# Proj's products split by seven a second time, and half of the exchange issued from GpSimd's queue

## The chip, the cores and the metric

The kernel runs on one core of a Trainium2 chip. The metric is device time in microseconds for one execution. TensorE is called PE (its weight loads PEld), VectorE DVE, ScalarE ACT, GpSimd POOL and SyncE SP.

## What is computed

A cross-attention block, all in fp32, for four batches of 512 queries and 512 context rows, width 512, 16 heads of 32, MLP width 2048:

```python
x = layer_norm(hidden_states, ln1_w, ln1_b)
q = x @ q_w + q_b;  k = ctx @ k_w + k_b;  v = ctx @ v_w + v_b
attn = softmax(q k^T / sqrt(32), masked)
hidden = (attn v) @ cproj_w + cproj_b + hidden_states
y = layer_norm(hidden, ln2_w, ln2_b)
y = gelu(y @ fc_w + fc_b)
return hidden + y @ proj_w + proj_b
```

## The kernel before

**An order written out.** The string ORDER holds some thousands of tokens, and a loop at the end issues them one after another. A token such as `P:0:5` names a step (here project, batch 0, product 5); a step that yields is taken up again where it stopped when its token comes again. Each engine works its instructions strictly in this order, and so do the DMA queues: `load` (L278) puts a DMA on SP's queue, `nc.gpsimd.dma_start` one on POOL's. The tiles of a Ring (`accs`, four PSUM banks; `stage`, two SBUF buffers; `rows_of`, six) are taken and given back in this order as well. `add` (L281) and `sub` (L284) are helpers, so sums of many places share these lines.

**Attention** runs over 16 groups w (batch and four heads) and four query tiles. Token `u` (L419) makes scores into four PSUM banks `sc`, `x` subtracts the minimum on DVE (L427) and exponentiates on ACT (L430), `r` transposes 32x32 blocks on DVE into `swap` (L438, L445). `e` is the exchange: for each half of a group 16 DMAs, each of a 32-partition block of 136 KB, put the transposed blocks into the partitions where `a` (attend, L470) needs them:

```python
for d in range(NI):
    for i in (0, 2, 1, 3):
        j = (i + d) % NI
        load(pT[ts(j, HD), i], tb[ts(i, HD), j])
    yield
```

Between these stand the products of k, q and v (L384, L396, L406) for later groups, c (cproj, L352), the layer norms (`s`, `r1`, `r2`, `n`, `t`) and fc.

**fc** (L528) is a Strassen-Winograd product: for each batch b and each of eight pairs c of blocks of 128 hidden columns (`f:b:c`) seven products in place of eight. `fs` makes the four sums of its weights on POOL (for the last batch `sw`, on DVE), `j` (fc_join) joins the seven results into a stage buffer, `g` applies gelu on ACT (L575). The result of the first three batches goes to DRAM (`gd`, L578, on POOL's queue) and comes back for proj; that of the last batch (`z`, `zj`, `zg`) stays in SBUF.

**proj** (`P:b:n`, L637) is 512 rows by 2048 by 512 for each batch, again in seven products n of 256x1024 by 1024x256: 16 matmul calls of 256 columns each. `ps` makes the weight sums once, `gs` the sums of the activations on DVE (the rows of L281 and L284 that name `swap` and `mix`), `J` (project_join) adds the results into the residual, which `hd` loads and to which `pb` adds the bias on POOL, and stores the output. Products 1, 2 and 6 use the ring of accumulators, the rest the four score banks, which are free by then.

An fp32 matmul call shows as two instructions in the profile.

Of the kernel before, what the change touches and what calls it, by code (L numbers as in the profile page):

```python
# [12 lines left out]
F32 = mybir.dt.float32  # L13
# [27 lines left out]

LN1W, LN1B, QB, KB, LN2W, LN2B, FCB = 0, 4, 8, 12, 16, 20, 24
# [24 lines left out]
u:2:0 k:4 e:1:0 e:1:0 e:1:0 r:1:3 s1:1 r1:1 n1:1 a:0:1 r:1:2 x:2:0 n1:1 n1:1 r:1:3 x:2:0 x:2:0 x:2:0 n1:1 r:1:3 k:5
u:2:1 x:2:1 wk:6 wq:4 wq:5 x:2:1 r:2:0 k:4 x:2:1 e:1:1 e:1:1 e:1:1 wk:7 e:1:1 v:4 x:2:1 r:2:0 t1:1:0
u:2:2 r:2:1 x:2:2 t1:1:1 t1:1:1 r:2:1 t1:1:0 x:2:2 r:2:1 r:2:1 x:2:2 x:2:2 v:5 t1:1:2 t1:1:2 a:1:0
u:2:3 a:1:0 x:2:3 v:5 t1:1:3 t1:1:3 x:2:3 q:5 a:1:1 r:2:2 x:2:3 x:2:3 r:2:2 r:2:3 a:1:1  # L70
u:3:0 k:6 k:6 x:3:0 r:2:3 r:2:3 x:3:0 r:2:3 x:3:0 x:3:0 q:5 e:2:0 wv:7 e:2:0 e:2:0 e:2:0 q:4
u:3:1 x:3:1 x:3:1 r:3:0 r:3:1 x:3:1 x:3:1 v:4 r:3:1 r:3:1 r:3:0 r:3:1 k:7
u:3:2 a:2:0 x:3:2 q:4 e:2:1 e:2:1 e:2:1 wq:7 e:2:1 a:2:0 e:3:0 e:3:0 e:3:0 x:3:2 x:3:2 wv:6 wq:6 e:3:0 x:3:2 v:7
u:3:3 q:7 r:3:2 r:3:2 x:3:3 x:3:3 a:2:1 x:3:3 x:3:3 r:3:3 r:3:3 v:7
u:4:0 m:1 x:4:0 x:4:0 x:4:0 x:4:0
u:4:1 r:3:3 a:2:1 r:3:3 k:7 x:4:1 e:3:1 e:3:1 x:4:1 r:4:0 x:4:1 x:4:1 r:4:1 r:4:1 r:4:0 e:3:1 e:3:1 r:4:1 q:6 a:3:0
  a:3:0
u:4:2 x:4:2 x:4:2 r:4:1 x:4:2 x:4:2 c:0:1 v:6
u:4:3 c:0:1 v:6 x:4:3 e:4:0 e:4:0 lh:0 e:4:0 e:4:0 lx:2 le:2 lh:0 le:2 le:2 wk:8 wv:8 le:2 r:4:2 c:0:0 x:4:3 x:4:3
  x:4:3  # L80
u:5:0 a:3:1 c:0:0 r:4:3 r:4:2 x:5:0 x:5:0 q:6 x:5:0 x:5:0 a:3:1 c:0:2 fs:0:0 cb:0 c:0:0 r:4:3 s2:0
u:5:1 r:4:3 c:0:2 v:4 v:5 cb:0 x:5:1 r:4:3 q:7 r:5:0 x:5:1 x:5:1 x:5:1 c:0:3 c:0:3 a:4:0
u:5:2 v:8 k:8 s2:0 s2:0 s2:0 r:5:1 r:5:0 a:4:0 c:0:1 fs:0:0 c:0:2 c:0:3 r2:0 x:5:2 x:5:2 n2:0 n2:0 n2:0 n2:0 t2:0:0
  t2:0:0 x:5:2 v:8 r:5:1 t2:0:1 x:5:2 t2:0:1
u:5:3 t2:0:3 t2:0:2 r:5:1 wk:9 e:4:1 x:5:3 t2:0:3 k:9 x:5:3 k:9 t2:0:2 r:5:1 s1:2 e:4:1 e:4:1 e:4:1 r:5:2 x:5:3 wv:9
  a:4:1 lh:1 x:5:3 r:5:2
u:6:0 r:5:3 a:4:1 x:6:0 k:8 y:0 y:0 lx:2 s1:2 lx:2 s1:2 lx:2 s1:2 y:0 e:5:0 wv:10 wq:8 e:5:0 e:5:0 e:5:0 wk:10 f:0:1
  v:9 f:0:0 v:9 j:0:0 r1:2 x:6:0 r:5:3 x:6:0 r:5:3 n1:2 n1:2 f:0:0 f:0:1 f:0:0 j:0:0 n1:2 n1:2 x:6:0 r:5:3 y:0 e:5:1
  e:5:1 lh:1 e:5:1 lf:0:4 wq:9
u:6:1 j:0:0 j:0:0 t1:2:2 x:6:1 j:0:1 t1:2:2 r:6:0 x:6:1 f:0:0 x:6:1 x:6:1 j:0:0 t1:2:0 t1:2:0 g:0:0 g:0:0 a:5:0  # L90
u:6:2 t1:2:1 r:6:0 a:5:0 j:0:1 r:6:1 k:10 x:6:2 t1:2:1 r:6:1 x:6:2 x:6:2 x:6:2 r:6:1 t1:2:3 f:0:1 t1:2:3
u:6:3 r:6:1 e:5:1 j:0:1 x:6:3 x:6:3 r:6:2 x:6:3 j:0:1 x:6:3 r:6:3 r:6:3 k:10 q:9 a:5:1 a:5:1 r:6:2
u:7:0 x:7:0 x:7:0 fs:0:3 g:0:0 fs:0:2 q:9 r:6:3 fs:0:2 f:0:2 fs:0:3 fs:0:1 fs:0:2 fs:0:2 f:0:2 f:0:1 j:0:2 x:7:0 x:7:0
  j:0:1 g:0:1 g:0:1 g:0:1 cb:1 fs:0:3 fs:0:3 r:6:3 j:0:2 lx:3 e:6:0 e:6:0 e:6:0 lf:0:4 e:6:0 f:0:3 f:0:2
u:7:1 f:0:2 j:0:2 j:0:2 j:0:2 g:0:2 g:0:2 g:0:2 v:6 x:7:1 x:7:1 r:7:0 j:0:3 r:7:0 q:8 f:0:3 x:7:1 x:7:1 j:0:3 a:6:0
u:7:2 v:7 r:7:1 a:6:0 x:7:2 v:10 x:7:2 x:7:2 q:8 r:7:1 r:7:1 v:10 x:7:2 r:7:1 e:6:1 lh:1 m:1 cb:1 fs:0:4 v:9 cb:1 v:8
  fs:0:4 fs:0:4 fs:0:4 e:6:1 e:6:1 e:6:1 r:7:2 wq:11 wv:11 e:7:0 wq:10
u:7:3 f:0:4 j:0:4 x:7:3 x:7:3 f:0:4 j:0:4 x:7:3 r:7:2 x:7:3 f:0:3 a:6:1
u:8:0 m:2 v:11 x:8:0 r:7:3 x:8:0 v:11 x:8:0 j:0:3 r:7:3 r:7:3 f:0:4 j:0:3 a:6:1 j:0:4 x:8:0 f:0:3
u:8:1 r:7:3 wk:11 lf:0:6 lf:1:0 e:7:0 e:7:0 e:7:0 lf:0:5 wv:13 lf:0:5 e:7:1 f:0:4 lh:1 e:7:1 q:10 wq:12 e:7:1 lf:0:7  # L100
  e:7:1 r:8:0 x:8:1 x:8:1 j:0:4 x:8:1 j:0:4 a:7:0 j:0:3 x:8:1
u:8:2 r:8:1 g:0:3 a:7:0 r:8:1 g:0:3 r:8:0 r:8:1 x:8:2 x:8:2 g:0:4 g:0:4 x:8:2 c:1:0 r:8:1 lf:0:7 lf:1:0 e:8:0 e:8:0
# [97 lines left out]
def xattn_block(ctx: ExitStack, tc: tile.TileContext, x, encT, mask, q_w, k_w, v_w, c_w, w_fc, p_w, vecs, rows, out):  # L200
# [577 lines left out]
```

## Time and profile before

| | |
|---|---|
| median of 3 runs | 791.18 us (789.69 to 792.59) |
| profiled execution | 789.92 us |
| its span | 788.1 us, granted clock 1.00 |
| busy in the span: PE, DVE, ACT, POOL | 778.2, 565.9, 361.0, 188.6 us |
| DMA | 158.16 MB, mean 201 GB/s |
| scores run | 22.9 to 502 us |
| first product of proj | 541 us |
| last matmul ends, last join | 785, 785.4 us |

Busy time of PE includes time in which matmuls wait in the pipeline, so 99% does not say that it is full. The chain of waits is the sequence of work that ended last, followed back from the last instruction. A group's row gives line, engine, operation, tiles out<-in, shapes and count, then busy us and mean ns of one, then idle us before it with what ended the idle time. A DMA on POOL's or SP's queue shows there with the time of its issue, and in the list of issues with the time until it landed.

### The profile page before, as it was taken

How to read it: one execution, taken by the hardware profiler on the slowest of the kernel's cores; microseconds unless marked ns; L12 is line 12 of the kernel's file. 1: busy time of each engine (PE TensorE's matmuls, PEld its weight loads, DVE VectorE, ACT ScalarE, POOL GpSimd, SP SyncE). 2: the span in 40 equal slices, each digit the busy share in tenths (PEclk: the TensorE clock that was granted, in tenths of full speed). 3: DMA queues.
4: the chain of work that ended last, by engine and by line, in shares of the span. 5: the costliest groups of instructions: out<-in, count | busy, mean ns of one | idle time of the engine just before them, and what ended most of it. 6: DMA issues, size and time to landing. Idle time of an engine off the chain costs nothing.

```text
span 788.1 us, 12510 instructions
## 1 busy us (share of the span) xinstructions
PE 778.2 (99%) x4370; PEld 538.2 (68%) x4370; DVE 565.9 (72%) x1145; ACT 361.0 (46%) x764; POOL 188.6 (24%) x230
## 2 busy tenths in 40 slices
PE   9998999999999999999999999999999999999998
PEld 6543653557566556665546677766888888888887
DVE  3788879899988799997889898844963248532631
ACT  2565755556865765859587777920000010112000
POOL 0141000220271133303232724400142600110411
PEclk9999999999999999999999999999999999999999
DMA  8988878898989989887977998899804602300003
GB/s 296 298 212 212 235 186 203 238 289 206 255 230 250 260 231 265 252 248 191 264 215 204 278 290 235 220 269 412 317 1 161 226 27 66 115 28 1 27 7 107
DMA packets 64031, 158.16 MB, mean 201 GB/s; under 512 B 12848, under 2 KB 17072, under 8 KB 62304
## 3 DMA queue, kind: packets, MB, share of 16 engines
q1 hardware_dynamic: 58992, 140.36, 63.2%
q0 software_dynamic: 4832, 16.98, 5.8%
q8 instruction: 35, 0.57, 0.3%
q14 instruction: 28, 0.23, 0.1%
q10 hardware_dynamic: 144, 0.02, 0.0%
HBM read 65.03 MB, written 20.97 MB: 109 GB/s over the span
## 4 chain that ended last, share of the span: by engine, by line
PE 91%; DMA 2%; DVE 2%; ACT 2%; SPq 2%; issue 0%; POOL 0%; DVEq 0%; POOLq 0%
PE acc L528 20%; PE sc L637 14%; PE acc L637 11%; PE sc L419 8%; PE acc L384 7%; PE acc L470 7%; PE acc L406 7%; PE acc L396 6%; PE acc L352 6%; PE sc L528 4%; PE acc L320 2%; DMA swap<-swap 2%; SPq L278 2%; DVE ptt L427 1%; ACT ptt L430 1%; DMA ext<-fc_w_dram 1%
## 5 line engine op out<-in xcount | busy, mean ns | idle before, releaser
L430 ACT ACTIVATE ptt<-ptt,mn 128x512 f32<-128x512 f32 x256 | 182.7, 715 | 105.9 <-DVE mn L427 105.2
L427 DVE CUSTOM_DVE_ANT_0 ptt<-sc,mix 128x512 f32<-128x512 f32 x256 | 165.4, 678 | 27.8 <-PE sc L419 23.6
L438 DVE STREAM_TRANSPOSE swap<-ptt 128x1024 f32<-128x1024 f32 x64 | 78.9, 1234 | 9.0 <-DMA pbt<-fc_w_dram 3.9
L419 PE MATMUL sc<-pbt 32*128 32x512 f32 x512 | 80.0, 640 | 1.6 <-ACT pbt L398 0.8
L445 DVE STREAM_TRANSPOSE swap<-ptt 128x1024 f32<-128x1024 f32 x64 | 77.9, 1222 | 1.2 <-ACT ptt L430 1.2
L470 PE MATMUL acc<-swap,mix 128*32 128x256 f32 x1024 | 61.9, 382 | 3.1 <-DMA swap<-swap 3.1
L406 PEld LDWEIGHTS acc<-ptt,ext 128*128 128x128 f32 x512 | 58.9, 192 | 7.0 <-issue 4.2
L528 PE MATMUL acc<-yT,pbt 128*128 128x256 f32 x240 | 62.5, 389 | 0.3 <-DVE st L281 0.2
L406 PE MATMUL acc<-ptt,ext 128*128 128x128 f32 x512 | 60.8, 277 | 0.0
L528 PEld LDWEIGHTS acc<-yT,pbt 128*128 128x128 f32 x240 | 43.4, 190 | 23.1 <-issue 9.8
L384 PE MATMUL acc<-ext,ptt 128*128 128x512 f32 x128 | 58.7, 604 | 0.0
L352 PE MATMUL acc<-mix 128*128 128x512 f32 x128 | 58.5, 599 | 0.1
L396 PE MATMUL acc<-ext,ptt 128*128 128x512 f32 x128 | 58.2, 599 | 0.0
L528 PE MATMUL acc<-ys,wsum 128*128 128x256 f32 x224 | 57.6, 379 | 0.3 <-DVE ys L284 0.3
L637 PE MATMUL acc<-pbt,swap 128*128 128x256 f32 x256 | 57.0, 379 | 0.0
L470 PEld LDWEIGHTS acc<-swap,mix 128*32 128x32 f32 x1024 | 30.2, 109 | 38.6 <-issue 9.9
L637 PEld LDWEIGHTS acc<-pbt,swap 128*128 128x128 f32 x256 | 48.6, 190 | 7.0 <-DVE mix L281 0.2
L281 POOL TENSOR_TENSOR xn<-xn,row 128x512 f32<-128x512 f32 x16 | 20.4, 1274 | 135.4 <-DMA xn<-x_dram 135.3
L281 DVE TENSOR_TENSOR st<-acc,st 128x512 f32<-128x512 f32 (+1 forms) x72 | 42.2, 593 | 12.9 <-PE acc L528 11.5
L654 ACT COPY mix<-acc 128x512 f32<-128x512 f32 x4 | 2.3, 586 | 100.0 <-PE acc L637 42.8
L430 ACT ACTIVATION_READ_ACCUMULATOR ptt<-ptt,mn 128x1 f32 x256 | 48.0, 188 | 0.0
L528 PEld LDWEIGHTS acc<-ys,wsum 128*128 128x128 f32 x224 | 42.5, 190 | 6.4 <-issue 0.7
(107 smaller groups left out, 1205.4 us busy)
## 6 DMA issues: line engine op xcount, KB each, us to landing
swap<-swap SPq DMA_DIRECT2D x512, 136.0 KB, 3.3
gd<-st POOLq DMA_DIRECT2D x24, 512.0 KB, 5.0
swap<-gd SPq DMA_DIRECT2D x12, 1024.0 KB, 8.1
pbt<-fc_w_dram SPq DMA_DIRECT2D x40, 256.0 KB, 4.7
xn<-x_dram SPq DMA_DIRECT2D x32, 256.0 KB, 4.1
ptt<-k_w_dram SPq DMA_DIRECT2D x16, 256.0 KB, 4.9
ext<-encT_dram SPq DMA_DIRECT2D x16, 256.0 KB, 5.1
ptt<-v_w_dram SPq DMA_DIRECT2D x16, 256.0 KB, 4.8
```

The costliest lines, as they stand in the source:

```text
L352: nc.tensor.matmul(acc, oT[:, g, ts(t, P)], wc[:, g, :], start=(g == 0), stop=(g == NG - 1))
L384: nc.tensor.matmul(acc, S["wk", w][:, d, :], eT[:, d, :], start=(d == 0), stop=(d == ND - 1))
L396: nc.tensor.matmul(acc, S["wq", w][:, d, :], xT[:, d, :], start=(d == 0), stop=(d == ND - 1))
L406: nc.tensor.matmul(acc[:, ts(t, P)], eT[:, d, ts(t, P)], S["wv", w][:, d, :], start=(d == 0), stop=(d == ND - 1),)
L419: nc.tensor.matmul(sc[h], S["qT", w][r, ts(qt, P)], S["kT", w][r, :], start=True, stop=True)
L427: nc.vector.tensor_tensor_reduce(out=s, in0=sc[h], in1=mb, scale=1.0, scalar=FMAX, op0=ALU.add, op1=ALU.min, accum_out=mn)
L430: nc.scalar.activation(s, s, AF.Exp, bias=mn, scale=-1.0, accum_out=S["sums", w][:, qt, h : h + 1])
L438: nc.vector.transpose(*two_heads[0])
L445: nc.vector.transpose(*two_heads[1])
L470: nc.tensor.matmul(av[ts(h, HD), : 2 * P].rearrange(shape, **kw), v[:, t, ts(h, HD)], p[t][h], start=(t == 0), stop=(t == NT - 1),)
L528: nc.tensor.matmul(o, x[:, k], y[:, k], start=(k == 0), stop=(k == 1))
L637: nc.tensor.matmul(q[:, t], a[c][:, ts(t, P)], w[:, c], start=(c == 0), stop=(c == NP - 1))
```

## The change

Proj's seven products are each split by seven once more, except three that stay plain: products 1 and 2 of batch 0 and product 4 of batch 3 (`PLAIN`). A split product is seven sub-products of 128x512 by 512x128, four matmul calls of 128 columns each, 28 calls in all. `xs` makes the four sums of its activations on DVE, `pt` (once for each n) those of its weights. `pj` joins the seven into a row buffer with one copy on ACT and four additions on DVE (`joins`, which fc_join now uses too), and `J` adds these buffers into the residual, all on DVE.

The sums of fc's output that proj's first level needs are made on POOL right behind gelu (`gs`, g_sums), in one buffer `gs`, and stored to DRAM with it, for all four batches: `gd` holds seven blocks instead of four, and `la` loads one of them, 1 MB, for each product, into one of four buffers `ga`. fc's last batch goes the way of the others, with its weight sums on POOL.

Of the exchange's 16 DMAs for each half, those that read partitions 64 to 127 (i of 2 and 3) go to POOL's queue.

ORDER is written anew from end to end. The bias row of proj is loaded late (`lr`) into the place of v's.

```diff
+AT = {1: 0, 7: 1, 2: 2, 4: 3, 5: 4, 6: 5, 3: 6}
...
+LATE = (LAST, 4)
+PLAIN = ((0, 1), (0, 2), LATE)
...
-    gd = [dram.tile([P, NP, 2, L], F32, tag=f"gd{b}", name=f"gd{b}") for b in range(LAST)]
+    gd = [dram.tile([P, 7, NP, HL], F32, tag=f"gd{b}", name=f"gd{b}") for b in range(B)]
...
         for d in range(NI):
             for i in (0, 2, 1, 3):
                 j = (i + d) % NI
-                load(pT[ts(j, HD), i], tb[ts(i, HD), j])
+                queue = nc.sync if i < 2 else nc.gpsimd
+                queue.dma_start(out=pT[ts(j, HD), i], in_=tb[ts(i, HD), j])
             yield
...
+    def joins(g, names, key, own):
+        q, n = lambda i: S[names[i], *key], g.shape[-1]
...
+        nc.scalar.copy(g[:, 1], q(0)[:, 0])
+        done(0)
+        yield
+        add(nc.vector, g[:, 0:4:3], q(1), g[:, 1:2].broadcast_to([P, 2, n]))
+        done(1)
+        yield
+        add(nc.vector, g[:, 1:3], q(2), g[:, 3:4].broadcast_to([P, 2, n]))
+        yield
+        add(nc.vector, g[:, 3], q(2)[:, 0], g[:, 2])
+        done(2)
+        yield
+        add(nc.vector, g[:, 1:3], q(3), g[:, 1:3])
+        done(3)
...
-        if b < LAST:
-            nc.gpsimd.dma_start(out=gd[b][:, c], in_=g)
-            stage.done("g", b, c)
+
+    def g_sums(b, c):
+        g = S["g", b, c].rearrange("p i (j l) -> p (i j) l", j=2)
+        a11, a21, a12, a22 = (g[:, i] for i in range(4))
+        yield from a_sums(nc.gpsimd, a11, a12, a21, a22, gs[:, 0], gs[:, 1], a21, gs[:, 2])
+        yield
+        nc.gpsimd.dma_start(out=gd[b][:, :4, c], in_=g)
+        stage.done("g", b, c)
+        nc.gpsimd.dma_start(out=gd[b][:, 4:, c], in_=gs)
...
-    def load_g(b, k):
-        load(ga[b % 2][k], gd[b][:, 2 * k : 2 * k + 2])
+    def load_g(b, n):
+        load(ga[TURN[b, n] % 4], gd[b][:, AT[n]])
...
+    def g_sums2(b, n):
+        a, s = g_terms(b, n)
+        return a_sums(nc.vector, *a, *s)
...
     def project(b, n):
...
+        if (b, n) in PLAIN:
+            a, w = ga[TURN[b, n] % 4], p_of(n)
+            for t in range(2):
...
+                for c in range(NP):
+                    nc.tensor.matmul(q[:, t], a[:, c, ts(t, P)], w[:, c], start=(c == 0), stop=(c == NP - 1))
+                yield
+            return
+        (a11, a12, _, a22), (s1, s2, s3, s4) = g_terms(b, n)
+        (b11, _, b21, b22), (t1, t2, t3, t4) = p_terms(n)
+
+        def product(o, x, y):
+            h = NP // 2
+            for c in range(h):
+                nc.tensor.matmul(o, x[:, c], y[:, c], start=(c == 0), stop=(c == h - 1))
...
+        product(bank(2, "p1")[:, 0], a11, b11)
+        yield
+        q = bank(3, "p26")
+        product(q[:, 0], a12, b21)
+        product(q[:, 1], s2, t2)
+        yield
+        q = bank(0, "p57")
+        product(q[:, 1], s3, t3)
+        product(q[:, 0], s1, t1)
+        yield
+        q = bank(1, "p34")
+        product(q[:, 0], s4, b22)
+        product(q[:, 1], a22, t4)
+
+    def result(b, n):
+        r = S["r", b, n] = rows_of.take("r", b, n)
+        if (b, n) in PLAIN:
...
+            nc.scalar.copy(r, q)
...
+        else:
+            yield from joins(r.rearrange("p (i n) -> p i n", i=4), ("p1", "p26", "p57", "p34"), (b, n), 2)
```

More of the change, by code (lines that the diff above doesn't have):

```diff
@@ L40 @@
 PX = PW + 2 * HD
+AT = {1: 0, 7: 1, 2: 2, 4: 3, 5: 4, 6: 5, 3: 6}
+TURN = {p: i for i, p in enumerate([(0, n) for n in (1, 2, 6, 5, 7, 3, 4)]
+                                   + [(b, n) for b in range(1, B) for n in (1, 6, 5, 7, 3, 2, 4)])}
+LATE = (LAST, 4)
+PLAIN = ((0, 1), (0, 2), LATE)
 LN1W, LN1B, QB, KB, LN2W, LN2B, FCB = 0, 4, 8, 12, 16, 20, 24
@@ L213, in xattn_block @@
     vec = const.tile([P, NVEC], F32, tag="vec", name="vec")
-    row = const.tile([P, 3, D], F32, tag="row", name="row")
+    row = const.tile([P, 2, D], F32, tag="row", name="row")
     nhalf = const.tile([P, NT], F32, tag="nhalf", name="nhalf")
@@ L262, in mlp_w @@
     def mlp_w(n):
-        buffer, n = (ext, n - IN_EXT) if n >= IN_EXT else (pbt, n % MW + MW)
+        buffer, n = (ext, n % MW) if n >= IN_EXT else (pbt, n % MW + MW)
         return buffer[:, n * D : (n + 1) * D].rearrange("p (d f) -> p d f", d=ND)
@@ L413, in prep_v @@
         yield
-        add(nc.gpsimd, v, v, row[:, 2, ts(w % NG, P)][:, None, :].broadcast_to([P, NT, P]))
+        add(nc.gpsimd, v, v, row[:, 1, ts(w % NG, P)][:, None, :].broadcast_to([P, NT, P]))
     def scores(w, qt):
@@ L509, in fc_w @@
     def fc_w(b, c):
-        return S["w", c] if b == LAST else [mlp_w(2 * (b * NP + c) + i) for i in range(2)]
+        return [mlp_w(2 * (b * NP + c) + i) for i in range(2)]
     def fc_s(b, c):
@@ L607, in p_bias @@
         for t in range(NT):
-            add(nc.gpsimd, hids[b % 2][:, t], hids[b % 2][:, t], row[:, 1, :])
+            h = hids[b % 2][t // 2][:, t % 2]
+            add(nc.gpsimd, h, h, row[:, 1, :])
             yield
-    def load_wa(c):
-        wa = stage.take("w", c).rearrange("p (i d f) -> p i d f", i=2, d=ND)
-        S["w", c] = [wa[:, i] for i in range(2)]
-        for i in range(2):
-            load(wa[:, i], w_fc[:, 2 * c + i, :, :])
-            yield
-    def g_sums(b, k):
-        a11, a12, a21, a22 = (ga[b % 2][k][:, :, i, j * HL : (j + 1) * HL] for j in range(2) for i in range(2))
-        c = slice(2 * k, 2 * k + 2)
-        return a_sums(nc.vector, a11, a12, a21, a22, gs[:, 0, c], gs[:, 1, c], a21, gs[:, 2, c])
@@ L623, in project @@
-    def project(b, n):
-        g11, g12, s3, g22 = ([ga[b % 2][c // 2][:, c % 2, i, j * HL : (j + 1) * HL] for c in range(NP)]
-                             for j in range(2) for i in range(2))
-        s1, s2, s4 = ([gs[:, i, c] for c in range(NP)] for i in range(3))
-        b11, t3, b21, b22 = (pb[:, :, k, j * HL : (j + 1) * HL] for k in range(2) for j in range(2))
-        t1, t2, t4 = (pt[:, i] for i in range(3))
-        a, w = {
-            1: (g11, b11), 2: (g12, b21), 3: (s4, b22), 4: (g22, t4), 5: (s1, t1), 6: (s2, t2), 7: (s3, t3)
-        }[n]
-        for t in range(2):
-            if n == 4 or t == 0:
-                q = halves(accs.take("P", b, n) if n in (1, 2, 6) else sc[{5: 0, 7: 1, 3: 2, 4: 3 - 3 * t}[n]])
-            S["qp", b, n, t] = q
-            for c in range(NP):
-                nc.tensor.matmul(q[:, t], a[c][:, ts(t, P)], w[:, c], start=(c == 0), stop=(c == NP - 1))
-            yield
@@ L640, in project_join, with load_row, p_of @@
-    def project_join(b, n):
-        h, q = hids[b % 2], S["qp", b, n, 0]
-        def hid(i, j):
-            return h[:, 2 * i : 2 * i + 2, j * HL : (j + 1) * HL]
-        def join(engine, i, j, src):
-            add(engine, hid(i, j), src, hid(i, j))
+    def load_row():
+        load(row[:, 1, :], rows[1:2, :].broadcast_to([P, D]))
+    def p_of(n):
+        k, j, i = {1: (0, 0, 0), 2: (1, 0, 0), 3: (1, 1, 0), 7: (0, 1, 0), 5: (None, 0, 0), 6: (None, 0, 1),
+                   4: (None, 0, 2)}[n]
+        return pt[:, i] if k is None else pb[:, :, k, j * HL : (j + 1) * HL]
@@ new lines, in quarters, with p_terms, p_sums2, g_terms @@
+    def quarters(a):
+        h, m = NP // 2, HL // 2
+        return [a[:, k * h : (k + 1) * h, j * m : (j + 1) * m] for k in range(2) for j in range(2)]
+    def p_terms(n):
+        b11, b12, b21, b22 = quarters(p_of(n))
+        s = ws[n - 1]
+        return (b11, b12, b21, b22), (s[:, 0], s[:, 1], ws3 if n == 4 else b12, s[:, 2])
+    def p_sums2(n):
+        b, t = p_terms(n)
+        return b_sums(nc.vector, *b, *t)
+    def g_terms(b, n):
+        a11, a21, a12, a22 = quarters(ga[TURN[b, n] % 4])
+        s = xs[TURN[b, n] % 2]
+        return (a11, a12, a21, a22), (s[:, 0], s[:, 1], a21, s[:, 2])
@@ new lines, in g_sums2, with project, bank @@
+    def g_sums2(b, n):
+        a, s = g_terms(b, n)
+        return a_sums(nc.vector, *a, *s)
+    def project(b, n):
+        if (b, n) in PLAIN:
+            a, w = ga[TURN[b, n] % 4], p_of(n)
+            for t in range(2):
+                if t == 0 or (b, n) == LATE:
+                    q = halves(accs.take("P", b, n, t))
+                S["qp", b, n, t] = q[:, t]
+                for c in range(NP):
[8 more added lines that the diff above has]
+                nc.tensor.matmul(o, x[:, c], y[:, c], start=(c == 0), stop=(c == h - 1))
+        def bank(i, name):
+            k = 2 * TURN[b, n] + i
+            q = S[name, b, n] = (accs.take(name, b, n) if i > 1 else sc[k % HG])[:, :HL].rearrange("p (j n) -> p j n", j=2)
+            return q
+        product(bank(2, "p1")[:, 0], a11, b11)
[11 more added lines that the diff above has]
+        product(q[:, 1], a22, t4)
@@ L649, in store, with done @@
         def store(i, j, ts_=range(2)):
             for t in ts_:
-                load(out[b, ts(2 * i + t, P), j * HL : (j + 1) * HL], hid(i, j)[:, t])
-        if n == 1:
-            nc.scalar.copy(p1p, q)
-            accs.done("P", b, n)
+                load(out[b, ts(2 * i + t, P), j * HL : (j + 1) * HL], h[i][:, t, j * HL : (j + 1) * HL])
+        def done(n):
+            rows_of.done("r", b, n)
+        if (b, n) == LATE:
+            for t in range(2):
+                o = h[1][:, t, :HL]
+                add(nc.vector, o, o, S["qp", b, n, t])
+                yield
+                store(1, 0, (t,))
+                yield
+        elif n == 1:
+            join(0, 0, n)
+        elif n == 6:
+            add(nc.vector, S["r", b, n], S["r", b, n], S["r", b, 1])
+            done(1)
@@ L673, in project_join @@
             yield
-            join(nc.gpsimd, 1, 0, u3p)
-        elif n == 3:
-            join(nc.vector, 0, 1, q)
-            yield
-            store(0, 1)
-        elif n == 2:
-            join(nc.vector, 0, 0, q)
-            accs.done("P", b, n)
-            yield
-            store(0, 0)
-        else:
-            for t in range(2):
-                add(nc.vector, hid(1, 0)[:, t], S["qp", b, n, t][:, t], hid(1, 0)[:, t])
-                yield
-                store(1, 0, (t,))
-                yield
+            join(1, 0, n)
+            done(n)
+        else:
+            i, j = {3: (0, 1), 2: (0, 0), 4: (1, 0)}[n]
+            join(i, j, n)
+            done(n)
+            yield
+            store(i, j)
     load_k, load_q, load_v = (weights(i) for i in "kqv")
@@ L709, in xattn_block @@
     accs.done("warm")
-    load(row, rows[None, :, :].broadcast_to([P, 3, D]))
+    load(row, rows[None, ::2, :].broadcast_to([P, 2, D]))
     load_mask(0, nc.sync)
```

365 lines of the change are left out of this document (192 added, 173 removed).

## The prediction

> **What bounds the kernel now.** I read the page first (busy times, then the chain), next the windows cut at the two places where the work changes, then the chain in order of time.
>
> ```profile
> span 788.1 us, 12510 instructions
> PE 778.2 (99%) x4370; PEld 538.2 (68%) x4370; DVE 565.9 (72%) x1145; ACT 361.0 (46%) x764; POOL 188.6 (24%) x230
> ...
> PE 91%; DMA 2%; DVE 2%; ACT 2%; SPq 2%; issue 0%; POOL 0%; DVEq 0%; POOLq 0%
> ```
>
> TensorE carries 91% of the chain. A busy PE is no proof of a full PE, so the windows come next: attention from 23 to 501, a short passage, the tail from 541 to 785, the end. Columns: length, busy time of PE, PEld, DVE, ACT, POOL with counts, granted clock, DMA share, GB/s.
>
> ```profile
> 23.00:501.00 478.00, 473.40 (x2919) 284.06 (x2920) 417.13 (x899) 322.94 (x701) 126.57 (x167) 1.00 0.87 238
> 501.00:541.00 40.00, 40.00 (x227) 25.88 (x226) 20.41 (x38) 15.41 (x26) 8.74 (x13) 1.00 0.95 298
> 541.00:785.00 244.00, 243.94 (x1138) 214.21 (x1136) 120.88 (x194) 17.95 (x32) 51.36 (x41) 1.00 0.30 105
> 785.00:788.00 3.00, 0.00 (x0) 0.00 (x0) 0.40 (x1) 0.00 (x0) 0.00 (x0) 1.00 0.13 44
> ```
>
> In the tail PE is full at clock 1.00, DVE half used, ACT and POOL nearly free, DMA at 0.30. Proj lies there, so a microsecond taken off proj's matmuls is one off the end, as long as DVE and POOL can feed it. In attention DVE is at 417 of 478 as well, so PE and DVE are both near their limit; POOL works 127 of 478.
>
> The chain in order of time gives the real pace, because its pieces abut:
>
> ```profile
> 129.86 0.51 SPq L278
> ...
> 142.05 2.40 DMA swap<-swap
> ...
> 315.09 3.57 PE acc L406 x32
> ...
> 544.91 6.91 PE sc L637 x32
> ...
> 784.98 0.42 DVE ext L281
> ```
>
> One of proj's products (L637) is 16 matmul calls of 256 columns, each two instructions in fp32: 32 in 6.91 us, 0.216 each. Prep of v (L406) is 16 calls of 128 columns in groups of four: 32 in 3.57 us, 0.112 each. The chain from 541 on is PE and nothing else until the last join at 784.98.
>
> **Part 1, the second split.** Of 28 products (seven in each of four batches) 25 are split; (0,1), (0,2) and (3,4) stay plain. A split one is seven sub-products of 128x512 by 512x128: 28 calls of 128 columns, in groups of four, the very form of L406. 56 instructions by 0.1116 are 6.25 us for 6.91, so 0.66 by 25: **16.5 us off PE**. The other end comes from the group means:
>
> ```profile
> L406 PE MATMUL acc<-ptt,ext 128*128 128x128 f32 x512 | 60.8, 277 | 0.0
> L406 PEld LDWEIGHTS acc<-ptt,ext 128*128 128x128 f32 x512 | 58.9, 192 | 7.0 <-issue 4.2 <-DMA swap<-swap 1.0 <-ACT ptt L430 0.8
> ```
>
> 60.8/512 is 0.119, hence 6.65 us and only 6.5 us saved. A weight load lasts 192 ns but 58.9/512 is 0.115 of busy time each: loads overlap, and at 128 columns loading and streaming are evenly matched. I take 16.5, since 3.57 is one undisturbed group and 60.8 holds breaks.
>
> **Part 2, DVE in the tail.** Rows for the prices:
>
> ```profile
> L284 DVE TENSOR_TENSOR swap<-swap 128x512 f32<-128x512 f32 x16 | 14.0, 885 | 0.0
> L281 DVE TENSOR_TENSOR mix<-swap 128x512 f32<-128x512 f32 x16 | 12.9, 819 | 3.3 <-DMA swap<-gd 3.3
> L284 DVE TENSOR_TENSOR mix<-swap,mix 128x512 f32<-128x512 f32 x16 | 12.7, 812 | 19.4 <-PE sc L637 19.4
> L284 DVE TENSOR_TENSOR mix<-mix,swap 128x512 f32<-128x512 f32 x16 | 12.3, 777 | 0.0
> L281 DVE TENSOR_TENSOR ext<-sc,ext 128x512 f32<-128x512 f32 x12 | 8.0, 686 | 14.8 <-PE sc L637 13.3 <-POOL ext L281 1.4
> L281 DVE TENSOR_TENSOR st<-acc,st 128x256 f32<-128x256 f32 x24 | 9.8, 410 | 0.3
> L284 DVE TENSOR_TENSOR wsum<-st,wsum 128x256 f32<-128x256 f32 x8 | 4.3, 538 | 0.1
> ```
>
> Added: 100 sums of activations (four for each split product, 512 elements) and 28 of weights, 128 by 0.69 is 88; the joins of 25 products, three adds of 256 by 0.41 and one of 128 that I put at half of that, 36; 43 joins into the residual of 512 by 0.69, 30. Gone: the 64 sums of the first four rows, 52; 24 joins of 512 and six of 256, 19; 32 weight sums of fc's last batch, priced at the last row, 17. Net 66: DVE goes from 121 in 244 us to 187 in some 227, 82%. It fits under PE, so I charge nothing; the cover is thin, since every PSUM bank of a product waits for DVE, in program order.
>
> ACT gains one copy of 128x128 for each of the 25 products and a 512 one for the plain two; it is busy 18 of 244 us there, so they cost nothing.
>
> **Part 3, POOL.** It takes 256 of the 512 exchange DMAs, four sums for each of 32 pairs of fc blocks, one DMA more for each, and fc's weight sums of the last batch; it loses 16 joins.
>
> ```profile
> L284 POOL TENSOR_TENSOR wsum<-wsum,pbt 128x256 f32<-128x256 f32 x20 | 14.6, 729 | 0.0
> ...
> L578 POOL DMA_DIRECT2D gd<-st x24 | 13.7, 571 | 76.4 <-ACT st L575 56.3 <-ACT mix L443 17.6 <-ACT p L554 2.5
> ...
> L281 POOL TENSOR_TENSOR ext<-mix,ext 128x512 f32<-128x512 f32 x16 | 23.0, 1453 | 81.7 <-DVE ext L281 58.1 <-DVE mix L281 23.4
> ...
> gd<-st POOLq DMA_DIRECT2D x24, 512.0 KB, 5.0
> ```
>
> 256 by 0.57 is 146; 128 sums by 0.73, 93; 40 DMAs by 0.57, 23; 32 weight sums by 0.73, 23; less 23. So 189 becomes 451, 58% of the span. The order is what matters: from u:13:0 to the last f:3 token POOL has 64 exchange DMAs, 19 groups of four sums with two DMAs each, 75 weight sums and some 23 smaller steps. By the rows that is 36 + 55 + 22 + 55 + 18, 186 us, while PE's tokens there sum to 206 us at the chain's pace: 90% of an engine that waits in order. Queued behind each wait of POOL (for a gelu, for a weight load) are now exchange copies, for which attend on PE waits, and weight sums, for which fc waits. Also gs is one buffer: a group of sums may start only when the last one's store has landed, 5.0 us by the row. I charge **8 us**; the ends are 0, if other POOL work fills each wait, and 30 (rival below).
>
> **Part 4, SP's relief.** The chain's piece from 129.86 to 142.05 is one exchange: 16 DMAs issued one after another in 12.2 us, and 2.4 until the last landed.
>
> ```profile
> L278 SPq DMA_DIRECT2D swap<-swap x512: 507/589/2165, 34.3 to 526.8; - x171
> ...
> PE acc L470 <- DMA swap<-swap: 3.1, 1, 3.1
> ```
>
> Eight from each queue would be out in about 5 us. But PE waits openly for an exchange once, 3.1 us, and SPq's 2% of the chain (16 us) have DVE close behind. I take **4 us off**; the ends are 0 and 12. In the Trainium skill, SBUF — State Buffer, "Can I just issue two DMAs to hit both halves?", it says that DMAs on the two halves of the partitions share the same engines, and two at once gained 6%. By that rule this gain is nearly 0 and the sum 4 us higher. No run so far has two exchanges from two queues.
>
> **Part 5, the rest.** DMA: stores of 896 KB for 32 pairs instead of 512 for 24, and 28 loads of 1 MB instead of 12, are 33 MB more on 158; two thirds falls into the tail, where the share is 0.30. In attention 20 pairs by 384 KB come to a share that is 0.87 already: 2 us, between 0 and 8. DVE against POOL:
>
> ```profile
> 575.94 1.75 DVE L284 TENSOR_TENSOR swap<-swap 128x512 f32<-128x512 f32 x1
> ...
> 580.70 0.68 DVE L284 TENSOR_TENSOR mix<-mix,swap 128x512 f32<-128x512 f32 x1
> ...
> 572.80 7.69 POOL L281 TENSOR_TENSOR ext<-ext,row 128x512 f32<-128x512 f32 x5
> ```
>
> While POOL adds (572.80 to 580.49), a DVE sum with both inputs in SBUF lasts 1.75 us, beside an idle POOL 0.68. In the tail after, POOL has about 86 us of such work, most of it ahead of the last f:3 token, where the order gives DVE some 44 such sums, 30 us, in 105 us of PE. Say it is a third of the time: such a sum runs at 0.39 of its pace, so 86 by 0.33 by 0.61 is 17 us more DVE, 204 of 227, still under PE. I charge 2, between 0 and 8.
>
> Sum: -16.5 + 8 - 4 + 2 + 2 is -8.5. The profiled execution took 789.92 (span 788.1 and 1.8 around it), so 781.4; it lies 1.3 under the median of the runs, 791.18, which makes **782.5** after rounding.
>
> **Rivals.** *POOL's queue sets the pace* (slower). POOL's share is 24% now and 90% from u:13:0 to f:3. For it: 76.4 us of waiting ahead of 24 stores, 3.2 each, and a store that takes 5.0 to land before gs is free. If each of the 19 groups there waits 2 us that nothing fills, 186 becomes 224, 18 over PE's 206; with weight sums, exchange copies and contention behind it another 8 in the earlier batches: 789.9 - 16.5 - 4 + 4 + 26 + 1.3 is 800.7, so 797 to 804. It decides from about 1 us of open wait for each group. Against it: the order was laid out anew, and the page gives POOL much waiting that costs nothing now.
>
> *The gain is eaten* (same): DVE at 90% holds PSUM banks a little too long in the last 130 us, 6 us, and POOL costs 10: 791.
>
> *The exchange was a brake all along* (faster): SPq and DMA together hold 4% of the chain, 32 us. If two queues give back 12 of it and POOL costs only 4, 789.9 - 16.5 - 12 + 4 + 4 + 1.3 is 770.7. Against it: in the open PE waited 3.1 us for an exchange.
>
> *Narrow matmuls don't pay* (slower): if a pass of 128 columns could not start before its own weight load of 0.190 us, a product would cost 56 by 0.19, 10.6 us, 3.7 more by 25: 875. The row of L406, 0.112, speaks against it. The Trainium skill, TensorE: Matmul & The Clock Gate, "Back-to-back issue gap", has 81 ns for 128 columns and 131 ns for 512 with weight loads between, so narrow passes are dearer per column; by that rule the split would lose. The trace disagrees for fp32, with 0.112 against 0.216 for twice the columns.
>
> *The exchange is not quicker from two queues*, all else as forecast: 786.5.
>
> **How the numbers follow.** The forecast has 0.43, its variant without the exchange's gain 0.08, the brake 0.07, eaten 0.09, POOL 0.30, narrow matmuls 0.03. About 0.3% (2.4 us) is what a measurement of this kernel can tell from no change. Faster: 0.43 + 0.08 + 0.07, less 0.01 of the edge, 0.57; same 0.09 and 0.01, 0.10; slower 0.33. The range, 769 to 802, leaves out narrow matmuls, the upper third of POOL's case and a little of the brake. The forecast's own range is 774 to 788.
>
> **What would show it.** Right: L637's successor at 56 instructions of 128 columns in 6.25 us; PE unbroken from the first product to the end, tail shorter by 16; DVE near 190 to 205 there; POOL near 450 in total. Wrong: PE or PEld waiting on POOL wsum, DMA swap<-swap or DVE st between u:13 and f:3 (POOL's case); PE waiting on DVE in the last 130 us (eaten); 0.19 us per narrow pass.

## The result and the profile after

The changed kernel takes **848.74 us** (median of 4 runs, 847.57 to 852.60), the kernel before beside it 790.45; the ratio is 1.0741 (95% interval 1.0699 to 1.0783). The forecast was 782.5.

The page of the kernel after (busy times, then the chain):

```profile
span 847.3 us, 14503 instructions
PE 791.1 (93%) x4970; PEld 556.5 (66%) x4970; DVE 641.5 (76%) x1290; ACT 374.5 (44%) x793; POOL 450.5 (53%) x670
...
PE 49%; DMA 15%; POOL 15%; DVE 8%; issue 5%; ACT 4%; SPq 3%; DVEq 0%; POOLq 0%; ACTq 0%
```

POOL's 450.5 us are the 451 of Part 3, and yet the chain has left PE: 91% became 49%, and POOL with the DMAs that it issues (and others) took 30%. PE stands still for 847.3 - 791.1 = 56.2 us instead of 9.9. Its busy time should have fallen by the 16.5 of Part 1 to 761.7; it rose to 791.1. So the 59.2 us of longer span are 46.3 more of standing still and 29.4 of busy time above 761.7, less the 16.5 saved.

Windows of the kernel after: attention until the scores end, the passage, the last part; then the stretch from the first score of `u:13:0` to the last instruction of fc. Columns as in the prediction.

```profile
26.00:546.00 520.00, 495.81 (x2956) 293.86 (x2957) 422.51 (x905) 333.75 (x712) 326.70 (x516) 0.98 0.88 240
546.00:700.00 154.00, 129.28 (x669) 103.56 (x666) 94.14 (x152) 30.87 (x56) 102.86 (x133) 0.93 0.64 208
700.00:844.00 144.00, 143.16 (x1237) 141.56 (x1235) 117.62 (x220) 5.23 (x20) 18.23 (x12) 0.99 0.56 197
...
416.00:675.00 259.00, 226.76 (x1183) 162.53 (x1175) 171.11 (x312) 110.50 (x202) 196.75 (x274) 0.94 0.76 229
```

Only the last 144 us look like the tail that was forecast: PE full, DVE at 118 of 144. The scores end at 546 instead of 502. The stretch of the last row was forecast at 186 us of POOL beside 206 of PE. POOL's work is about as forecast, 197, but the stretch lasts 259, with PE busy in 227 of them at a granted clock of 0.94. POOL is 76% busy there, and it still sets the pace.

How it does that, first in the groups of POOL in this stretch (one row for the first of the four sums, one for the second store):

```profile
L322 POOL TENSOR_TENSOR mix<-st 128x256 f32<-128x256 f32 x20 | 16.4, 819 | 40.2 <-ACT st L617 20.0 <-DMA gd<-mix 18.0 <-DVE st L322 2.2
...
L627 POOL DMA_DIRECT2D gd<-mix x19 | 14.4, 756 | 0.0
```

The 40.2 us of waiting ahead of the first sums are for a gelu (ACT, 20.0), for the last store of `gs` (18.0) and for a join (2.2). Then one piece of the stretch: the timeline of POOL, then one row of the chain, one row of ACT's timeline (the second half of the gelu), and PE's timeline. Columns are start, length, engine, line, operation, and in brackets the wait before it:

```profile
609.42 0.75 POOL L627 DMA_DIRECT2D gd<-mix  x1
612.26 1.13 POOL L322 TENSOR_TENSOR wsum<-ext 128x256 f32<-128x256 f32 x1 [2.10 <-PE sc L570]
613.47 0.73 POOL L325 TENSOR_TENSOR ext<-ext 128x256 f32<-128x256 f32 x1
617.42 1.15 POOL L322 TENSOR_TENSOR mix<-st 128x256 f32<-128x256 f32 x1 [3.22 <-ACT st L617]
...
622.44 0.75 POOL L627 DMA_DIRECT2D gd<-mix  x1
623.20 0.73 POOL L325 TENSOR_TENSOR wsum<-wsum,ext 128x256 f32<-128x256 f32 x1
```

```profile
609.42 6.90 DMA gd<-mix
```

```profile
616.61 0.73 ACT L617 ACTIVATE st<-st,vec 128x512 f32<-128x512 f32 x1
```

```profile
609.34 1.10 PE L570 MATMUL acc<-ys,wsum 128*128 128x256 f32 x4
...
620.67 1.03 PE L570 MATMUL acc<-yT,ext 128*128 128x256 f32 x4
623.99 2.08 PE L570 MATMUL acc<-ys,wsum 128*128 128x256 f32 x4 [2.29 <-POOL wsum L325]
```

POOL makes two of four weight sums of fc (612.26, 613.47). The next instruction in its queue is the first sum of a gelu's output, 617.42, which writes `gs`. It needs two things. `gs` is still being stored until the DMA issued at 609.42 lands 6.90 us later, at 616.32, and the gelu's second half ends at 617.34. POOL stands for 3.22 us; the gelu ends last here, as the view says, though the chain goes back over the store. Then come the four sums and both stores, and only then the third weight sum, which needed neither the gelu nor `gs`, at 623.20. PE has been out of work since 621.70 and waits 2.29 us for it. That is one instance of the rival "POOL's queue sets the pace", step by step.

The wait costs more than its length. Windows of 2 us around it (the third number from the right is the granted clock):

```profile
622.00:624.00 2.00, 0.01 (x1) 0.01 (x1) 0.27 (x1) 0.72 (x1) 1.99 (x4) 0.94 0.77 273
624.00:626.00 2.00, 2.00 (x5) 1.64 (x6) 0.00 (x0) 0.55 (x2) 1.92 (x3) 0.50 0.88 295
626.00:628.00 2.00, 2.00 (x8) 1.65 (x7) 1.73 (x3) 0.44 (x1) 1.04 (x2) 0.71 0.42 108
628.00:630.00 2.00, 2.00 (x11) 1.75 (x10) 2.00 (x3) 0.00 (x0) 1.92 (x3) 1.00 0.58 164
```

PE comes back at half its clock, 0.50; the 0.71 is the mean of a window in which the clock returns to 1.00, some 3 us after the restart. PE gets through 5 and 8 matmuls in 2 us, then 11 again. The span has nine such stretches at half clock, of 3.4, 6.8 or 10.2 us, 47.8 us together; PE is busy in 37.5 of them, so by an estimate from these numbers they cost half of that, 18.8 us, of the 29.4 above. The other 10.6 stay open. The mean clock of the span is 0.972, in the kernel before 1.00.

A pause does not always bring this. In the kernel before PE stood 3.13 us for an exchange, until 66.42 us, and its clock stayed at 1.00:

```profile
64.00:66.00 2.00, 0.00 (x0) 0.00 (x0) 0.61 (x3) 1.75 (x6) 0.00 (x0) 1.00 1.01 250
66.00:68.00 2.00, 1.58 (x32) 1.13 (x32) 1.55 (x2) 0.00 (x0) 0.00 (x0) 1.00 1.09 250
```

The Trainium skill, TensorE: Matmul & The Clock Gate, "HAM oscillation — how this bites in real kernels", has the same effect, the clock halved after TensorE idles, and gives gaps of over about 3.4 us as the condition. The trace agrees on the half, but shows it after 2.29 us. What decides when a pause brings it, these runs don't show.

### The profile page after: what moved, and what is told of

Same layout as the page of the kernel before. It is cut to its first block, busy times and chain, and to the rows that moved or that the text cites. A ratio compares the mean times of both kernels' runs of the same rounds, so it can differ in the third digit from the quotient of the medians.

```text
span 847.3 us, 14503 instructions
## 1 busy us (share of the span) xinstructions
PE 791.1 (93%) x4970; PEld 556.5 (66%) x4970; DVE 641.5 (76%) x1290; ACT 374.5 (44%) x793; POOL 450.5 (53%) x670
## 4 chain that ended last, share of the span: by engine, by line
PE 49%; DMA 15%; POOL 15%; DVE 8%; issue 5%; ACT 4%; SPq 3%; DVEq 0%; POOLq 0%; ACTq 0%
PE sc L707 9%; DMA gd<-mix 7%; PE acc L707 6%; PE acc L447 5%; PE sc L460 5%; PE acc L570 5%; PE acc L437 5%; PE acc L425 5%; PE acc L512 4%; POOL mix L325 3%; DMA xn<-x_dram 2%; DMA swap<-swap 2%; SPq L499 2%; POOL mix L322 2%; DVE ptt L468 2%
## 5 line engine op out<-in xcount | busy, mean ns | idle before, releaser
L468 DVE CUSTOM_DVE_ANT_0 ptt<-sc,mix 128x512 f32<-128x512 f32 x256 | 165.0, 680 | 29.4 <-PE sc L460 25.1
L499 POOL DMA_DIRECT2D swap<-swap x256 | 127.9, 505 | 73.9 <-DVE swap L489 22.2
L322 DVE TENSOR_TENSOR st<-acc,st 128x512 f32<-128x512 f32 (+1 forms) x104 | 64.0, 620 | 45.1 <-ACT st L594 19.4
L460 PE MATMUL sc<-pbt 32*128 32x512 f32 x512 | 86.4, 643 | 5.5 <-DVE mn L468 5.4
L322 POOL TENSOR_TENSOR mix<-st 128x256 f32<-128x256 f32 x32 | 25.4, 793 | 92.8 <-ACT st L617 56.9
L594 ACT COPY xn<-acc 128x128 f32<-128x128 f32 x25 | 6.5, 266 | 149.7 <-PE acc L707 95.5
L570 PE MATMUL acc<-ys,wsum 128*128 128x256 f32 x224 | 60.7, 395 | 8.2 <-POOL wsum L325 6.4
L512 PE MATMUL acc<-swap,mix 128*32 128x256 f32 x1024 | 64.7, 396 | 3.8 <-ACT st L594 1.8
L617 ACT ACTIVATE st<-st,vec 128x512 f32<-128x512 f32 x64 | 43.8, 717 | 52.2 <-DVE st L322 49.6
L322 POOL TENSOR_TENSOR ext<-ext,row 128x512 f32<-128x512 f32 x8 | 11.9, 1500 | 98.3 <-DMA ext<-xa 98.3
L512 PEld LDWEIGHTS acc<-swap,mix 128*32 128x32 f32 x1024 | 31.4, 113 | 40.7 <-issue 10.6
```

Of the source, the lines that this page charges most:

```text
L322: engine.tensor_tensor(o, x0, x1, ALU.add)
L460: nc.tensor.matmul(sc[h], S["qT", w][r, ts(qt, P)], S["kT", w][r, :], start=True, stop=True)
L468: nc.vector.tensor_tensor_reduce(out=s, in0=sc[h], in1=mb, scale=1.0, scalar=FMAX, op0=ALU.add, op1=ALU.min, accum_out=mn)
L499: queue.dma_start(out=pT[ts(j, HD), i], in_=tb[ts(i, HD), j])
L512: nc.tensor.matmul(av[ts(h, HD), : 2 * P].rearrange(shape, **kw), v[:, t, ts(h, HD)], p[t][h], start=(t == 0), stop=(t == NT - 1),)
L570: nc.tensor.matmul(o, x[:, k], y[:, k], start=(k == 0), stop=(k == 1))
```

## The experiments

Times are medians of 4 runs; the kernel before beside them was at 788.88 (first four), 788.68 (next four) and 789.62 us (last four), so a difference between medians of different sets carries 1 to 2 us of this; the runs of one kernel spread by up to 10 us. The theories, numbered 1 to 4: the single buffer `gs` is what makes POOL wait; POOL's queue as such has too much in it, in strict order; the exchange copies suffer on POOL's queue; and, added for the second four, the sums hold fc's two stage buffers longer.

**The sums left out** (a_nosums). `gs` is a constant, both stores stay.

```diff
-        yield from a_sums(nc.gpsimd, a11, a12, a21, a22, gs[:, 0], gs[:, 1], a21, gs[:, 2])
+        yield
+        yield
+        yield
```

> The changed kernel without the four POOL sums of each group (gs is set to zero once, the stores stay, proj reads wrong sums): POOL is 102 us lighter and gs has no wait. Theory 1: no more than 10 us below the kernel whose stores don't read gs. Theory 2: far below it, 785 to 800. Theory 3: 830 or more.

Measured 799.17 us, ratio 1.0113 (1.0076 to 1.0149). So the four sums for each pair, 101 us of POOL's time, cost 49.6 us of the kernel's. In the profiled executions the span is 50.8 us shorter: PE stands still for 33.5 us less and is busy for 17.3 less. The waits of the kernel after, and of this one, for the weight sums:

```profile
PEld acc L570 <- POOL wsum L325: 16.9, 6, 6.4
PE acc L570 <- POOL wsum L325: 12.0, 3, 5.6
```

```profile
PEld acc L570 <- POOL wsum L325: 2.3, 2, 1.5
PE acc L570 <- POOL wsum L325: 1.1, 1, 1.1
```

12.0 us in three waits of PE become 1.1 in one; the rest of the 33.5 is spread over many smaller waits, for DVE and ACT above all.

**`gs` never waits** (a_gsfree). The second store reads three quarters of the gelu's buffer instead of `gs`, so what it stores is other data; everything else stays.

```diff
-        nc.gpsimd.dma_start(out=gd[b][:, 4:, c], in_=gs)
+        nc.gpsimd.dma_start(out=gd[b][:, 4:, c], in_=g[:, :3])
```

> The changed kernel, but the second store of each group reads the stage buffer and not gs: same bytes and queue, no store ever reads gs, so a group of sums never waits for the last group's store (proj then reads wrong sums). Theory 1, gs as a single buffer is the brake (the chain has DMA gd<-mix 7%, about 60 us): 800 us or less, the waits of POOL mix for DMA gd<-mix (33.5 us) gone. Theory 2, POOL's load in order is the brake: 835 to 848, the waits move elsewhere. Theory 3, the exchange from POOL lands late: 835 to 848.

836.17 us, 1.0595 (1.0565 to 1.0626): the single buffer is worth 12.6 us, and not the 48 or more that Theory 1 expected. The wait moved on to the buffer that is now stored twice; first the rows of the kernel after, then of this one:

```profile
ACT st L594 <- DMA gd<-st: 42.9, 15, 8.6
POOL mix L322 <- DMA gd<-mix: 33.5, 8, 8.5
```

```profile
ACT st L594 <- DMA gd<-st: 53.6, 15, 8.2
```

**All copies back on SP** (a_xsp).

```diff
-                queue = nc.sync if i < 2 else nc.gpsimd
-                queue.dma_start(out=pT[ts(j, HD), i], in_=tb[ts(i, HD), j])
+                load(pT[ts(j, HD), i], tb[ts(i, HD), j])
```

> The changed kernel with all 16 exchange copies of a half on SP's queue again, order as it is: POOL is 128 us lighter. Theory 1: within 10 us of 848, since gs still waits. Theory 2: 800 to 825. Theory 3: 800 to 825, and the copies land in 3.3 us again instead of 5.2.

846.37 us, 1.0716 (1.0672 to 1.0759). POOL falls from 450.5 to 324.5 us busy and the time by 2.4, which the scatter of the runs covers. The 800 to 825 of Theories 2 and 3 did not come. Beside the sums the copies' place is worth next to nothing, and POOL's busy time alone is no measure of its harm.

**The split exchange alone, in the kernel before** (b_xpool). The same two lines, put into the kernel before.

> The kernel before with the copies out of the upper 64 partitions issued from POOL's queue, nothing else: the change's second part alone, where POOL has 189 us of other work. Theories 1 and 2: 782 to 793, little either way. Theory 3: 800 or more, with copies that land in 5 us.

857.70 us, 1.0875 (1.0845 to 1.0906). Waits of this run:

```profile
POOL swap L458 <- DVE swap L448: 54.8, 5, 20.2
DVE swap L438 <- DMA swap<-swap: 43.3, 10, 11.5
PE acc L471 <- DMA swap<-swap: 25.1, 6, 7.7
```

POOL is busy 313.0 us there, 37% of the span, but a copy waits in its queue behind whatever POOL waits for, and the reverse: PE waited 3.1 us for copies before, 25.1 here, and 9.2 us for `wsum` where it waited for none. The copies land in 5.2 and 5.5 us. That is what Theory 3 expected; Theories 1 and 2 missed by 65 us. In an order that wasn't written for it the same two lines cost 69 us, in the rewritten order 2.4 at most (the run before this one).

**A third stage buffer** (a_stage3). The store doesn't read `gs`, its place becomes a third buffer of the stage, and all four sums are written over one quarter of the gelu's output (their values are lost).

> The changed kernel with stores that don't read gs, and a third stage buffer in gs's place (the sums are written over one block of the stage buffer, so proj reads wrong sums). To be read against the kernel without the third buffer, 836. Theory 4: 805 to 818, and ACT's wait for DMA gd<-st (53.6 us there) goes. Theory 2: 830 or more.

838.64 us, 1.0630 (1.0593 to 1.0667), no better than without the third buffer (836.17). ACT's 53.6 us of waiting for the stores are gone, and the time stays, as Theory 2 expected: so the stage buffers aren't the cause. PE now waits 8.3 us for `wsum` and 7.2 for ACT.

**The gelu's store earlier** (a_early). It is issued behind the second of the four sums, once the quarter that is overwritten is ready.

> The changed kernel with the store of the stage buffer issued behind the second of the four sums, the last that writes it, instead of behind the fourth; it computes the reference. Theory 4: the buffer comes free about 1.6 us sooner in each of 32 groups, 835 to 843. Theory 2: 846 to 849.

849.01 us, 1.0762 (1.0736 to 1.0788): nothing, again against Theory 4.

**The last batch's sums on DVE** (a_dve3).

```diff
-        yield from a_sums(nc.gpsimd, a11, a12, a21, a22, gs[:, 0], gs[:, 1], a21, gs[:, 2])
+        yield from a_sums(nc.vector if b == LAST else nc.gpsimd, a11, a12, a21, a22, gs[:, 0], gs[:, 1], a21, gs[:, 2])
```

> The changed kernel with the sums of the last batch's eight groups on DVE (0.41 us each instead of 0.79); it computes the reference. Theory 4: the stretch in which the last batch's fc is the only source of stage buffers gets shorter, 830 to 842. Theory 2: about the same, 835 to 845, because POOL is 25 us lighter there. If DVE is the bound in the tail: slower than 848.

860.95 us, 1.0909 (1.0879 to 1.0938), 12 more, which only the last of the three expectations allowed. In this order DVE passes the wait on, it doesn't take it over: PE waits once for 12.1 us on a sum of DVE, where it waited 6.4 in the changed kernel.

**Sums that nobody waits for** (a_private). The same count and size of sums, on a tile `cz` of their own; the store of the gelu's output goes out ahead of them, and `gs`, which is stored behind them, is a constant. The sums' results are not used.

```diff
-        yield from a_sums(nc.gpsimd, a11, a12, a21, a22, gs[:, 0], gs[:, 1], a21, gs[:, 2])
-        yield
         nc.gpsimd.dma_start(out=gd[b][:, :4, c], in_=g)
+        yield from a_sums(nc.gpsimd, *[cz] * 8)
+        yield
         stage.done("g", b, c)
         nc.gpsimd.dma_start(out=gd[b][:, 4:, c], in_=gs)
```

> The changed kernel, but POOL's four sums of each group work on a tile of their own (same shape, same place in the order), the store of gelu's result is issued ahead of them, and the store of the sums sends a constant (proj reads wrong sums). POOL keeps its 102 us of sums, but they hold neither a stage buffer nor gs. Theory 2, POOL's own time: 830 to 848. Theory 4, the two stage buffers are held too long (join, gelu, sums, store until landed) and each next join waits for one on ACT: 795 to 808, like the kernel without sums (799).

824.07 us, 1.0435 (1.0394 to 1.0477). It lies between the ranges of Theories 2 and 4. So of the 49.6 us half, 24.9, are there although the sums need nothing and hold nothing: they only take their turn in POOL's queue. The other half, 24.7, goes with what they wait for and what they hold; the 12.6 of the run in which `gs` never waits are of this kind. A little of it is that these sums are shorter, 86 us in all for 101. The page's busy times, here and without sums, speak to one more cause, POOL's sums slowing DVE's:

```profile
PE 786.7 (95%) x4970; PEld 554.7 (67%) x4970; DVE 642.1 (78%) x1290; ACT 373.6 (45%) x793; POOL 440.2 (53%) x672
```

```profile
PE 773.8 (97%) x4970; PEld 548.6 (69%) x4970; DVE 640.4 (80%) x1290; ACT 373.8 (47%) x793; POOL 356.0 (45%) x543
```

DVE is busy 642.1 against 640.4, so that is not where the 24.9 us come from. It isn't always so: in the next pair, with all copies on SP, DVE is busy 647.0 us with the sums and 635.7 without.

**Which job behind the sums pays?** Four runs, from the two kernels just named: all copies on SP, once without sums (c_nosums_xsp) and once with the sums that nobody waits for (c_private_xsp); then with fc's weight sums left out, `wsum` a constant (c_nosums_nofs, c_private_nofs).

```diff
     def w_sums(engine, b, c):
-        x, y = fc_w(b, c)
-        return a_sums(engine, x[:, :2], x[:, 2:], y[:, :2], y[:, 2:], *fc_s(b, c))
+        yield
+        yield
+        yield
```

> Leaves out the four POOL sums of each fc block (as the run without sums did) and puts all exchange copies back on SP; POOL then has about 230 us of work. Theory (POOL's queue is too full and too strictly ordered in this order): without the sums POOL has slack enough, so the exchange's place matters little: 795 to 801 beside the 799 with the copies on POOL. Rival (POOL's 127 us of issuing is itself the rest of the loss above the forecast): 780 to 788. Rival (two queues do help once POOL is free): slower, 805 or more.

> The sums run on a tile of their own that nothing waits for (their results are not used), stores go out ahead of them, and all exchange copies are back on SP. Beside 824 with the copies on POOL. Theory A (the sums cost through the exchange copies that stand behind them in POOL's queue): 800 to 808. Theory B (through the weight sums that stand behind them): 820 to 826.

> The sums run on a tile of their own, stores go out ahead of them, and fc's weight sums on POOL are left out (wsum is set once; fc's result is then another). Theory B (the sums delay the weight sums for which fc waits): 797 to 806, near the run without weight sums and without activation sums. Theory A (the sums delay the exchange copies): 815 to 824.

> Leaves out both the activation sums and fc's weight sums on POOL; the base line for the run before it. If POOL still holds anything up in the run without activation sums (799) it falls to 785 to 793; if POOL has slack there, it stays within 3 us of 799.

| | no sums | sums that nobody waits for | the sums' cost |
|---|---|---|---|
| copies on both queues | 799.17 | 824.07 | 24.9 |
| copies on SP alone | 809.39 | 820.47 | 11.1 |
| copies on both queues, no weight sums | 799.33 | 804.08 | 4.8 |

The ratios of the last four are 1.0276 (1.0216 to 1.0337), 1.0407 (1.0342 to 1.0472), 1.0180 (1.0125 to 1.0235) and 1.0124 (1.0088 to 1.0159). Both times with sums fell where B expected them, and A's two ranges were missed. But beside its own kernel without sums the first says more: taking the copies out of POOL's queue removes 13.8 of the 24.9, taking the weight sums out 20.1, more together than there is, so neither path alone carries the cost. Two of the three jobs (sums, copies, weight sums) nearly fit into the queue, three don't: without sums the weight sums cost nothing (799.17 and 799.33).

The third expectation of c_nosums_xsp came true instead of the first: with POOL free of sums, the two queues do help, by 10.2 us. The chain of that run, all copies on SP, then of the one with both queues and no weight sums (that of the run with weight sums can be followed only in part):

```profile
PE 63%; DVE 11%; DMA 10%; SPq 9%; ACT 3%; issue 3%; POOL 0%; DVEq 0%; ACTq 0%
```

```profile
PE 79%; DMA 10%; DVE 6%; ACT 2%; issue 1%; SPq 1%; POOL 0%; DVEq 0%; ACTq 0%
```

SP's issuing is 9% of the one and 1% of the other; the two differ in the weight sums as well.

## Why the prediction was wrong

**The step that failed is Part 3's charge of 8 us**, the term for POOL's queue, with its upper end of 30. The sums alone cost 49.6 us. The pieces were named, the wait behind a weight load or a gelu, `gs` until its store has landed, weight sums and copies behind it. The term was mis-sized in two ways. The stretch with 186 us of POOL beside 206 of PE lasted 259: 197 of work, 40.2 of waiting ahead of the first sums of the groups (20 by 2.0, the rival's figure), and some 22 of other waits, which were counted as filled. And the clock was not in the sum at all: 18.8 us by the estimate above, some 8 of which are there without the sums too. That POOL's waiting "costs nothing now" was no argument: in the kernel before PE waits for POOL only once, 1.3 us at the start, and that says nothing of work which is yet to be put behind those waits.

POOL's load of 451 us, measured 450.5, was right by luck. The exchange copies took 127.9 us and not 146, the sums 101 and not 93, and a store holds POOL for 0.76 to 0.80 us and not 0.57, 13 us more in all; the errors cancel.

**The rival "POOL's queue sets the pace"** was the case that happened. Of the waits listed for it under "What would show it" the one on `wsum` is there, 12.0 us of PE; PE hardly waits for `swap<-swap` or for DVE's `st`, where the waits are one step earlier, of DVE for copies and of ACT for stores. Its 797 to 804 had the right mechanism and charged 26 us for POOL, half of what the sums alone cost.

**Part 1** was right. A row of the chain after, in the last part, where PE hardly pauses:

```profile
705.18 3.57 PE sc L707 x32
```

32 instructions of 128 columns take the 3.57 us that L406 promised. The rival "narrow matmuls don't pay" and the rule beside it fall for fp32. (Its 875 was a slip: it still has the 16.5 us in it that it would not have gained, and is 891.5 by its own terms.) At that pace the 16.5 us are saved, but the sums alone lose three times as much.

**Part 2** was right: without the sums the tail has DVE at 189 us in 233, with 187 in some 227 forecast. Its charge of nothing held as well: PE is busy in 228.9 of the 230 us until its last matmul ends at 793.0.

```profile
563.00:796.00 233.00, 228.86 (x1727) 216.91 (x1725) 189.03 (x332) 23.18 (x55) 63.30 (x67) 1.00 0.58 205
```

**Part 4** was right only where POOL has room: 4 us taken off, 10.2 measured without sums, and with them nothing that the scatter doesn't cover (-2.4). Rows of the kernel after beside the 3.3 us of before:

```profile
swap<-swap SPq DMA_DIRECT2D x256, 136.0 KB, 5.2
swap<-swap POOLq DMA_DIRECT2D x256, 136.0 KB, 5.2
```

Each copy lands 1.9 us later when two queues issue them. The Trainium skill's rule that was weighed there, that such DMAs share the same engines (SBUF — State Buffer, "Can I just issue two DMAs to hit both halves?"), fits these rows. The gain of 10.2 us then is from issuing; SP's 9% of the chain speaks for that, but no run separates it.

**Part 5** was right on the bytes, 33.7 MB more. Its 17 us more of DVE for 86 us of POOL's work were too many: with the 101 us of sums DVE's busy time rose by 1.1 (641.5 against 640.4), though by 11.3 in the pair with all copies on SP. What either cost in time was not measured by itself.

**What stays open.** Without the sums the kernel is at 799.17, where Parts 1, 4 and 5 give 789.92 - 16.5 - 4 + 4 + 1.3 = 774.7; with the 10.2 that Part 4 measured the gap is 6 us wider. By its page PE stands still for 796.5 - 773.8 = 22.7 us, 12.8 more than before, and is busy for 12.1 more than 761.7, some 8 of it by half clock (PE is busy in 15.9 us of such stretches; the mean clock is 0.989). It isn't the weight sums (799.33 without them) nor the copies on POOL (809.39 without them). Whether it is the order itself wasn't tried. No version that was run beats the kernel before.

## What to carry to other kernels

An engine with half its time free isn't free for work that has to happen between two waits: in a queue worked in order, price what stands behind each new wait and who needs it next, and add the waits to the work (197 us of work stood for 259), instead of going by the busy share. A buffer that a DMA must empty is part of that wait, but freeing it here gave back 12.6 of 49.6 us, and buffers further down nothing. When the bound engine begins to pause, look at its clock behind the pauses as well: here that was about 18.8 us beside 46.3 of more standing still.

## What the runs showed of the hardware that was not expected

After a pause of 2.29 us TensorE came back at a granted clock of 0.50 and was at 1.00 again some 3 us later, while a pause of 3.13 us in the kernel before left it at 1.00. All stretches at half clock in the kernel after lasted 3.4, 6.8 or 10.2 us. A copy of 136 KB between partitions takes POOL 0.505 us to issue, and over all runs lands in 4.6 to 5.6 us (medians) from either of two queues in use, in 3.2 to 3.5 when SP issues all of them. In fp32 a pass of 128 columns with its weight load takes 0.112 us, one of 256 columns 0.216.
